# Last two sequences staged like the others, last unit's gates put off, and the first weight loads and transposes reordered, in an attention and mixture-of-experts kernel on one core

## Chip, core and metric

The kernel runs on one core of a Trainium2 chip. The metric is the time of one execution in microseconds (us) on the device. The kernel before was timed in three runs: 684.95, 686.94 and 687.5 us, median 686.94 us. A profiled execution of it took 678.78 us.

Names used below: PE is TensorE (matmuls and transposes; PEld is its weight load), DVE is VectorE, ACT is ScalarE, POOL is GpSimd, SP is SyncE, which here only issues DMAs. ACT and POOL issue DMAs as well.

## What is computed

Input x has 8 sequences of 512 tokens with 256 features, all in f32. The reference, cut to what matters:

```
x = x + attention(layernorm(x))
x = x + ffn(layernorm(x))

attention(x): q = x Wq; k = x Wk; v = x Wv
  scores = where(causal, q k^T, -inf)
  return softmax(scores / sqrt(256)) v

ffn(x): shared = (silu(x sg^T) * (x su^T)) sd^T            # 512 hidden
  probs = sigmoid(x router^T + bias)                       # 8 experts
  scores, indices = top_k(probs, 2); scores /= sum(scores)
  combined = sum over the two experts of score * expert(x) # same form as shared
  return shared + combined
```

So every token goes through causal attention within its sequence, through one shared expert, and through 2 of 8 routed experts.

## The kernel before, in words

**Order of the work.** `fold_qk` (L280 to L313) first loads Wq and Wk, transposes them on PE (L297, copied out by ACT at L298) and multiplies them (L307), so that scores are x (Wq Wk^T) x^T. Then the loop `for b in range(B)` (L630) does the sequences. In its stage, sequence b gets its attention products and second normalisation, and in the same stage the scores and values of sequence b+1 are computed (pm of L395 and L407, sc of L442) and the routing of sequence b is done. Then come the routed experts (`expert_up` L888, matmuls L900; `expert_down` L918, matmuls L923) over tiles of rows that were gathered by expert, and last the sums.

**Attention of one chunk.** A sequence has four chunks of 128 queries. `attend` (L458) takes the exponentials of a chunk transposed and multiplies them with v (`av`, L472), adds the result to the residual (`summed`, on DVE, L476, out `total`), and takes the statistics (L172 to L178 on DVE, `rstd` on POOL, L179); `normalize` (L325) writes the rows `hn` of the chunk before.

**Two ways of transposing.** PE can transpose a 128x128 block against the identity (L463 for the exponentials `ex`, `turned` with L340 for rows of hn), and ACT copies the result from PSUM to SBUF. Or SP writes the rows to DRAM, loads them back as blocks or squares of 32 (`stored_rows`, `loaded_blocks`, `loaded_squares`), and DVE transposes the blocks (`turn_squares` L384, `turn_exponentials` L434). Which sequence goes which way is set by three constants:

- `VIA = [b for b in range(B) if b != B - 2]`: their hn goes through DRAM, at least the first half.
- `WHOLE = range(B - 2)`: the second half of hn goes through DRAM too.
- `SENT = range(1, B - 1)`: their exponentials go through DRAM.

So before the change the hn of sequences 0 to 5 goes through DRAM, that of sequence 6 is transposed by PE, that of sequence 7 half and half, and the exponentials of sequences 0 and 7 are transposed by PE. `LATE` are sequences 4 to 6, whose shared expert is done at the end of the kernel from a copy of hT in DRAM (`hTd`).

**Units of the shared expert.** `shared_beside` (L564) does one unit: half a sequence, with 16 gate and up matmuls (pg, L578), the activation (tanh on ACT, two products on DVE at L593 and L596) and 8 down matmuls (po, L605). In the profile each of these matmuls is two rows. The units of sequences 0 to 3 and of sequence 7, ten in all, fill PE where the attention would make it wait. Before the change one unit lies in each of the stages of sequences 0 to 5, one beside the last sequence's routing (`added`), and three come after it and before the routed experts.

**Routing.** `chosen` (L754) holds a sequence's routing in steps, which `shared_beside` calls at the places named in `steps`: `turned` for what PE transposes, then `route` (L486): logits `lT` (L492), their transpose `pl` (L500), sigmoid, two maxima with their masks, and running counts `run` (L535). `places_of` (L540, PE at L544 and L545, out `pp`, then DVE to `at`, L554) gives each token its row, and `dispatch` (L557) writes a chunk's rows to `rows_h` by indirect DMAs from POOL, eight in each sequence.

**What sets the order.** `tc.issue_after(x)` puts the instructions below it behind x in the order of the program; on one engine they are then queued behind x. It adds no wait of its own. Each engine runs its queue in order, and buffers do the rest: `ps_o` has two PSUM buffers for lT, pl, po, av and pp, `ps_m` four for pm, sc and pg, `ps_t` two for transposes.

**The routed experts' inputs.** `fetch_w` (L831) loads the expert weights from ACT's queue, `fetch` (L841) the tiles `h` (L851) and `tail` (L856) from SP's queue; the first of these waits until the last dispatch has landed. `turn` (L873) transposes h on DVE for L900.

## Time and profile before

| What | Value |
|---|---|
| median of the timed runs | 686.94 us (684.95 to 687.5) |
| profiled execution, time | 678.78 us |
| profiled execution, span of the core | 677.0 us |
| DVE busy | 301.9 us (45%) |
| POOL busy | 157.2 us (23%) |
| ACT busy | 149.6 us (22%) |
| gate and up matmuls of routed experts, L900 | 896 rows, 211.6 us |
| down matmuls of routed experts, L923 | 448 rows, 101.4 us |
| gate and up matmuls of the units, L578 | 320 rows, 73.8 us |
| all DMA traffic | 119.52 MB, mean 177 GB/s |

The profile is one execution on the chip. A row of a group has the line, the engine, the operation, out<-in by the program's names, the shape and the count; then the busy time and the mean of one. A row of a timeline starts with its start in us from the span's start and its length; in brackets stands how long the engine was idle before it, and what ended that. Matmul rows overlap a little, since they are pipelined, so the cost of a row is better read from one start to the next.

### The profile page before, as it was taken

How to read it: one execution, taken by the hardware profiler on the slowest of the kernel's cores; microseconds unless marked ns; L12 is line 12 of the kernel's file. 1: busy time of each engine (PE TensorE's matmuls, PEld its weight loads, DVE VectorE, ACT ScalarE, POOL GpSimd, SP SyncE). 2: the span in 40 equal slices, each digit the busy share in tenths (PEclk: the TensorE clock that was granted, in tenths of full speed). 3: DMA queues.
4: the chain of work that ended last, by engine and by line, in shares of the span. 5: the costliest groups of instructions: out<-in, count | busy, mean ns of one | idle time of the engine just before them, and what ended most of it. 6: DMA issues, size and time to landing. Idle time of an engine off the chain costs nothing.

```text
span 677.0 us, 10380 instructions
## 1 busy us (share of the span) xinstructions
PE 663.7 (98%) x3170; PEld 542.0 (80%) x3170; DVE 301.9 (45%) x1004; ACT 149.6 (22%) x357; POOL 157.2 (23%) x210
## 2 busy tenths in 40 slices
PE   7999999999999999999999999999999999999998
PEld 5677787777776888888888888888888899984556
DVE  4678879779786853212212212122122112223665
ACT  3433231332223222121111111211111111111110
POOL 3103351533526520022112121111211122120000
PEclk9999999999999999999999999999999999999999
DMA  7665777867834367776555354463543457714775
GB/s 237 192 166 147 219 210 178 220 180 209 218 115 134 106 163 226 230 199 209 162 167 170 119 180 150 138 180 127 161 161 102 159 172 239 259 65 146 244 226 177
DMA packets 155529, 119.52 MB, mean 177 GB/s; under 512 B 111856, under 2 KB 134000, under 8 KB 155472
## 3 DMA queue, kind: packets, MB, share of 16 engines
q1 hardware_dynamic: 136272, 58.05, 32.8%
q10 hardware_dynamic: 12912, 43.53, 18.5%
q0 software_dynamic: 6288, 17.24, 7.0%
q8 instruction: 28, 0.46, 0.3%
q14 instruction: 29, 0.24, 0.1%
HBM read 83.31 MB, written 35.47 MB: 175 GB/s over the span
## 4 chain that ended last, share of the span: by engine, by line
PE 78%; DVE 9%; DMA 6%; SPq 2%; issue 2%; POOL 1%; ACT 1%; ACTq 0%; DVEq 0%; POOLq 0%
PE po L923 17%; PE pg L900 16%; PE pu L900 16%; PE pg L578 7%; PE po L605 4%; PE pg L1011 3%; PE po L1070 3%; PE pu L1011 3%; PE av L472 3%; PE sc L442 2%; PE pm L407 2%; PE pm L395 2%; SPq L377 2%; DVE bnst L172 2%; DMA blocks<-hnd 2%
## 5 line engine op out<-in xcount | busy, mean ns | idle before, releaser
L886 DVE TENSOR_TENSOR hidp<-pu,sgt 128x512 f32<-128x512 f32 x56 | 38.5, 690 | 209.2 <-PE pu L900 194.4
L929 POOL DMA_INDIRECT rows_y<-y,to x56 | 53.6, 957 | 263.7 <-ACT y L928 155.2
L900 PE MATMUL pg<-hTt,w 128*128 128x256 f32 x448 | 105.8, 379 | 0.0
L900 PE MATMUL pu<-hTt,w 128*128 128x256 f32 x448 | 105.8, 379 | 0.0
L923 PE MATMUL po<-w_down,hidp 128*128 x448 | 101.4, 379 | 0.9 <-ACT y L928 0.9
L923 PEld LDWEIGHTS po<-w_down,hidp 128*128 128x128 f32 x448 | 85.0, 190 | 12.8 <-ACT y L928 1.4
L900 PEld LDWEIGHTS pg<-hTt,w 128*128 128x128 f32 x448 | 85.1, 190 | 11.6
L900 PEld LDWEIGHTS pu<-hTt,w 128*128 128x128 f32 x448 | 85.1, 190 | 11.6
L578 PE MATMUL pg<-hT,w_sh 128*128 128x256 f32 x320 | 73.8, 382 | 0.2 <-issue 0.2
L559 POOL DMA_INDIRECT rows_h<-hn,at x64 | 62.9, 983 | 22.7 <-issue 17.1
L885 ACT ACTIVATE sgt<-pg 128x512 f32<-128x512 f32 x67 | 39.8, 598 | 125.8 <-PE pg L900 122.2
L578 PEld LDWEIGHTS pg<-hT,w_sh 128*128 128x128 f32 x320 | 59.7, 190 | 9.5 <-ACT sg L589 1.0
L928 ACT COPY y<-po 128x256 f32<-128x256 f32 x67 | 24.9, 373 | 156.0 <-PE po L923 142.9
L179 POOL TENSOR_TENSOR rstd<-var,minus_half 128x1 f32<-128x1 f32 (+1 forms) x43 | 27.0, 636 | 125.7 <-DVE var L178 77.1
L605 PE MATMUL po<-w_sh,hid 128*128 128x256 f32 x160 | 37.5, 384 | 0.2
L442 PE MATMUL sc<-xT,qT 128*128 128x128 f32 (+3 forms) x128 | 37.4, 434 | 0.0
L605 PEld LDWEIGHTS po<-w_sh,hid 128*128 128x128 f32 x160 | 29.2, 190 | 6.8 <-DVE hid L596 2.5
L395 PE MATMUL pm<-xT,w_qk 128*128 128x512 f32 x64 | 30.1, 592 | 0.0
L886 DVE TENSOR_TENSOR khid<-pu,sgt 128x512 f32<-128x512 f32 x11 | 7.6, 691 | 49.2 <-PE pu L900 49.2
L407 PE MATMUL pm<-wv_sb,xT 128*128 128x256 f32 x128 | 29.0, 380 | 0.2 <-ACT xT L341 0.2
L407 PEld LDWEIGHTS pm<-wv_sb,xT 128*128 128x128 f32 x128 | 24.2, 190 | 6.1 <-issue 2.6
L172 DVE BATCH_NORM_STATS2 bnst<-total 128x6 f32<-128x256 f32 x64 | 25.1, 409 | 8.3 <-DMA total<-in_x_dram 8.3
(156 smaller groups left out, 755.7 us busy)
## 6 DMA issues: line engine op xcount, KB each, us to landing
w<-in_gate_w_dram ACTq DMA_DIRECT2D x41, 512.0 KB, 3.4
w<-in_up_w_dram ACTq DMA_DIRECT2D x41, 512.0 KB, 4.7
yl<-rows_y SPq DMA_DIRECT2D x32, 256.0 KB, 4.0
h<-rows_h SPq DMA_DIRECT2D x112, 64.0 KB, 3.3
w_down<-in_down_w_dram SPq DMA_DIRECT2D x8, 512.0 KB, 4.6
out_dram<-total SPq DMA_DIRECT2D x32, 128.0 KB, 2.7
total<-in_x_dram SPq DMA_DIRECT2D x7, 512.0 KB, 7.0
hnd<-hn SPq DMA_DIRECT2D x13, 256.0 KB, 2.2
```

What stands on the lines that cost most here:

```text
L395: nc.tensor.matmul(pm, lhsT=w_qk[:, k, ts(m, P)], rhs=xT[:, k, :], start=(k == 0), stop=(k == ND - 1),)
L407: nc.tensor.matmul(pm, lhsT=xT[:, k, ts(c, P)], rhs=wv_sb[:, k, :], start=(k == 0), stop=(k == ND - 1),)
L442: nc.tensor.matmul(sc[:, :n], lhsT=qT[:, k, ts(i, P)], rhs=xT[:, k, :n], start=(k == 0), stop=(k == ND - 1),)
L559: lands(nc.gpsimd.indirect_dma_start(out=rows_h[:, :], out_offset=bass.IndirectOffsetOnAxis(ap=at[:, r, c : c + 1], axis=0), in_=hn[:, c, ...
L578: mm = nc.tensor.matmul(pg[:, w, :], lhsT=w_sh[:, ds(w * gu + k * I + m * P, P)], rhs=hT[:, k, at], start=(k == 0), stop=(k == ND - 1),)
L605: nc.tensor.matmul(po, lhsT=hid[:, m, ts(j, P)], rhs=w_sh[:, ds(2 * gu + m * D, D)], start=(m == 0), stop=(m == NI - 1),)
L885: nc.scalar.activation(sg, pg, AF.Silu)
L886: return nc.vector.tensor_tensor(out=hid, in0=pu, in1=sg, op=ALU.mult).ins
L900: nc.tensor.matmul(dst[:, m, :], lhsT=w[:, i, k, ts(m0 + m, P)], rhs=hT[:, ts(k, n * P)], start=(k == 0), stop=(k == ND - 1),)
L923: nc.tensor.matmul(po, lhsT=hid[:, m, ts(j, P)], rhs=w_down[:, ds(w + m * D, D)], start=(m == 0), stop=(m == NI - 1),)
L929: nc.gpsimd.indirect_dma_start(out=rows_y[:, :], out_offset=bass.IndirectOffsetOnAxis(ap=to[:, j : j + 1], axis=0), in_=y, in_offset=None,)
L1011: nc.tensor.matmul(dst, lhsT=w_sh[:, ds(off + k * I + m * P, P)], rhs=hT[:, k, :], start=(k == 0), stop=(k == ND - 1),)
```

## The change

The change has four parts.

1. The three constants become `range(7)`, `range(7)` and `range(1, 8)`: hn of sequence 6 and the exponentials of sequence 7 go through DRAM and DVE like those of the others, and hn of sequence 7 is transposed wholly by PE. With this the stage of sequence 6 has the same order as those before it: its normalisation, its second maximum, its steps of routing and a unit of the shared expert. `project_q` is skipped where there is no next sequence, and the last sequence keeps `placed` at chunk 2. One of the ten units lies in the stage of sequence 6 now, so that two instead of three are left after the last routing.
2. The unit beside the last sequence has its gates on DVE put behind the last `summed` (`gates_behind`), and the matmuls behind the first pair of it are put behind the last av (`halfway` moves from the place (1, 1) to (0, 1)).
3. The first half of the columns of Wk is loaded from ACT's queue instead of SP's. SP then has the first half of Wq and goes on with x; ACT has the second half of Wq and both halves of Wk.
4. PE does the four transposes of Wq first and then the four of Wk, instead of two and two in turn.

```diff
--- before.py
+++ after.py
@@ -73,9 +73,9 @@
     assert B == E, "each sequence's attention has one expert's down weights loaded beside it"
     EARLY = B // 2
     LATE = range(EARLY, B - 1)
-    VIA = [b for b in range(B) if b != B - 2]
-    WHOLE = range(B - 2)
-    SENT = range(1, B - 1)
+    VIA = range(B - 1)
+    WHOLE = range(B - 1)
+    SENT = range(1, B)
 
     BLOCKS = NT * (NT - 1) // 2, NT
     RS = 1.0 / D ** 0.5
@@ -283,7 +283,8 @@
             for n, w in (("q", wq), ("k", wk)):
                 t = beside.tile([P, ND, D], F32, tag="hT", name=f"w{n}", bufs=3)
                 loaded.append(t)
-                for k, queue in enumerate((nc.sync, nc.scalar)):
+
+                for k, queue in enumerate((nc.sync if n == "q" else nc.scalar, nc.scalar)):
                     columns = ts(k, P)
                     queue.dma_start(
                         out=t[:, :, columns], in_=w.rearrange("(p c) e -> p c e", c=ND)[:, :, columns]
@@ -294,9 +295,11 @@
                 pt = ps_t.tile([P, ND, D], F32, tag="t", name="pt")
                 for k in range(ND):
                     for c in range(ND):
-                        begun = nc.tensor.transpose(pt[:, k, ts(c, P)], t[:, c, ts(k, P)], ident).ins
+                        with nullcontext() if n == "q" else tc.issue_after(turned_q):
+                            begun = nc.tensor.transpose(pt[:, k, ts(c, P)], t[:, c, ts(k, P)], ident).ins
                     copied = nc.scalar.copy(tT[:, k, :], pt[:, k, :])
                 if n == "q":
+                    turned_q = begun
                     with tc.issue_after(copied.ins):
                         nc.scalar.dma_start(out=wv_sb, in_=wv.rearrange("(p c) e -> p c e", c=ND))
                 turned.append(tT)
@@ -479,7 +482,7 @@
             stats_of(mv, xb[:, i, :], i)
             power = rstd_of(rstd[:, i : i + 1], mv[:, i : i + 1, :])
             if i:
-                with tc.issue_after(summed.ins) if i != NT // 2 or xb is not total[B - 1] else nullcontext():
+                with tc.issue_after(summed.ins):
                     normalize(hn[:, i - 1, :D], xb, i - 1, mv, rstd)
             return mixed.ins, summed.ins, power
 
@@ -510,7 +513,7 @@
                 top, hot = tops[r][:, here], hots[r][:, here, :]
                 if r:
                     yield
-                with tc.issue_after(marks["turned"]) if r and b < B - 2 else nullcontext():
+                with tc.issue_after(marks["turned"]) if r and b < B - 1 else nullcontext():
                     nc.vector.tensor_reduce(out=top, in_=prob, axis=AX.X, op=ALU.max)
                 nc.vector.tensor_tensor(
                     out=hot, in0=prob, in1=top.unsqueeze(2).to_broadcast(wide), op=ALU.is_equal
@@ -561,7 +564,7 @@
                     in_=hn[:, c, :], in_offset=None,
                 ))
 
-        def shared_beside(b, half, hT, midway=None, behind=None, rows_from=NI, early=None, steps=(), halfway=None):
+        def shared_beside(b, half, hT, midway=None, behind=None, rows_from=NI, early=None, steps=(), halfway=None, gates_behind=None):
 
 
             n = S // 2
@@ -583,13 +586,14 @@
                         with tc.issue_after(mm.ins):
                             next(early, None)
                             held = marks["routed"]
-                    elif (m, w) == (NI // 2 - 1, 1) and halfway is not None:
+                    elif (m, w) == (0, 1) and halfway is not None:
                         held = halfway
                 sg = beside.tile([P, n], F32, tag="sg", name="sg")
                 nc.scalar.activation(sg, pg[:, 0, :], AF.Tanh, scale=0.5)
-                with nullcontext() if early is None or not 0 < rows_from < NI and m < rows_from else tc.issue_after(
-                    marks["half"] if m >= rows_from else marks["coming"]
-                ):
+                first = marks["half"] if m >= rows_from else marks["coming"]
+                if early is None or not 0 < rows_from < NI and m < rows_from:
+                    first = gates_behind
+                with nullcontext() if first is None else tc.issue_after(first):
                     nc.vector.scalar_tensor_tensor(
                         out=sg, in0=sg, scalar=1.0, in1=pg[:, 0, :], op0=ALU.add, op1=ALU.mult
                     )
@@ -661,7 +665,7 @@
                 rest = None
                 if b in SENT:
                     sc = exs[i]
-                    if i % 2 == 0:
+                    if i % 2 == 0 and ahead_T is not None:
                         with tc.issue_after(mixed) if i else nullcontext():
                             qT = project_q(ahead_T, range(i // 2 * ND // 2, (i // 2 + 1) * ND // 2), qT if i else None)
                 elif i + 1 < NT:
@@ -692,7 +696,7 @@
                     with tc.issue_after(summed):
                         added()
                     added = None
-                if i == (1 if b in SENT else 2) and placed is not None:
+                if i == (1 if b in SENT and ahead_T is not None else 2) and placed is not None:
                     placed()
 
 
@@ -760,7 +764,7 @@
                 next(routing)
                 yield
                 next(routing)
-                if b < B - 2:
+                if b < B - 1:
                     yield
                 mask = next(routing)
 
@@ -773,11 +777,8 @@
             if b + 1 < B:
                 choice = chosen()
                 next(choice)
-                if b + 2 == B:
-                    for _ in choice:
-                        pass
             else:
-                added = shared_beside(*waiting.pop(0), early=chosen(), rows_from=0, halfway=mixed, steps=((NI // 2, 1), (NI - 1, 0), (NI - 1, 1)))
+                added = shared_beside(*waiting.pop(0), early=chosen(), rows_from=NI, halfway=mixed, gates_behind=summed, steps=((NI // 2, 1), (NI - 1, 0), (NI - 1, 1)))
             if b in LATE:
                 with tc.issue_after(marks["sent"]):
                     nc.sync.dma_start(out=hT_d[b], in_=hT)
@@ -785,27 +786,26 @@
                 waiting += [(b, 0, hT), (b, 1, hT)]
             if b + 1 < B:
 
-                if b + 2 < B:
-                    def behind():
-
-                        nonlocal exT
-                        with tc.issue_after(marks["hid"]), tc.issue_after(marks["first"]):
-                            exT = turn_exponentials(squares)
-                        next(choice, None)
-                        marks["squares"], marks["turned"] = marks["turned"], marks["run"]
-
-                    def midway():
-                        if b + 3 < B:
-                            with tc.issue_after(marks["squares"]):
-                                rows, _ = first_norm(*coming)
-                            with tc.issue_after(marks["sent"]):
-                                blocks[b + 3], _ = sent_to_blocks(xn_d[b + 3], rows)
-
-                    added = shared_beside(
-                        *waiting.pop(0), midway=midway, behind=behind, early=choice,
-                        rows_from=1 if b in WHOLE else NI,
-                        steps=((NI // 2, 1), (NI - 1, 1)) if b in WHOLE else ((0, 1), (1, 1)),
-                    )
+                def behind():
+
+                    nonlocal exT
+                    with tc.issue_after(marks["hid"]), tc.issue_after(marks["first"]):
+                        exT = turn_exponentials(squares)
+                    next(choice, None)
+                    marks["squares"], marks["turned"] = marks["turned"], marks["run"]
+
+                def midway():
+                    if b + 3 < B:
+                        with tc.issue_after(marks["squares"]):
+                            rows, _ = first_norm(*coming)
+                        with tc.issue_after(marks["sent"]):
+                            blocks[b + 3], _ = sent_to_blocks(xn_d[b + 3], rows)
+
+                added = shared_beside(
+                    *waiting.pop(0), midway=midway, behind=behind, early=choice,
+                    rows_from=1 if b in WHOLE else NI,
+                    steps=((NI // 2, 1), (NI - 1, 1)) if b in WHOLE else ((0, 1), (1, 1)),
+                )
                 xT = ahead_T
         placed()
         for c in to_send:
```

## The prediction

> **What bounds the kernel now.** I read the page's first lines, then the waits of TensorE (PE), then the timeline of PE from 170 us to 290 us (where the change works) beside VectorE (DVE), GpSimd (POOL) and SyncE (SP), and last the first 13 us.
>
> The first line of the page and its row of granted clock:
>
> ```profile
> PE 663.7 (98%) x3170; PEld 542.0 (80%) x3170; DVE 301.9 (45%) x1004; ACT 149.6 (22%) x357; POOL 157.2 (23%) x210
> PEclk9999999999999999999999999999999999999999
> ```
>
> PE is the bound: 663.7 of 677.0 us. All its idle time is 13.3 us, so a change can win only by taking PE work out or by emptying some of these 13.3 us, and it loses where PE gets a new wait. The waits of PE (total us, times, longest):
>
> ```profile
> PE pt L297 <- DMA wq<-in_wq_dram: 4.0, 1, 4.0
> PE po L923 <- ACT y L928: 0.9, 1, 0.9
> PE pt L463 <- ACT ex L451: 0.7, 2, 0.4
> PE pl L500 <- ACT logits L497: 0.4, 1, 0.4
> PE pp L545 <- DVE run L535: 0.3, 1, 0.3
> PE lT L492 <- ACT hT L341: 0.2, 1, 0.2
> ```
>
> The last four stand in the stage that the change rewrites (sequence 7 under the routing of sequence 6, 198 to 217 us): by the timeline 0.20 + 0.39 + 0.31 + 0.39 = 1.29 us. The rest of the idle time is outside it. From PE's timeline (start, us, operation):
>
> ```profile
> 198.06 0.61 PE L442 MATMUL sc<-xT,qT 128*128 128x128 f32 x4
> 201.96 1.10 PE L340 MATMUL pt<-ident,hn 128*128 128x128 f32 x8
> 203.26 0.43 PE L492 MATMUL lT<-hT,r_sb 128*32 128x128 f32 x8 [0.20 <-ACT hT L341]
> 214.26 0.66 PE L463 MATMUL pt<-ident,ex 128*128 128x128 f32 x4 [0.39 <-ACT ex L451]
> 217.48 3.62 PE L578 MATMUL pg<-hT,w_sh 128*128 128x256 f32 x16
> 255.97 3.62 PE L605 MATMUL po<-w_sh,hid 128*128 128x256 f32 x16
> 259.42 1.89 PE L900 MATMUL pg<-hTt,w 128*128 128x256 f32 x8
> ```
>
> 217.48 is where the last attention product ends; call it T0. 259.42 is the first routed expert. Between them PE has only shared units (half a sequence of the shared expert), the last sequence's transposes and its routing. From start to start a row of 128x256 costs 0.216 us, a unit (32 pg rows, 16 po rows) 6.91 + 3.45 = 10.36 us.
>
> **The change, part by part.**
>
> 1. *Transposes.* The four groups of L463 go (start to start 0.26, 0.28, 0.33, 0.49: 1.36 us); the eight of sequence 6's hn go (1.10); sequence 7's hn takes eight instead of four (+0.47, the four at 220.93 to 221.40). Sum **-1.99 us** of PE work. In their place come DVE transposes and SP's transfers: hnd, four blocks, two exd, eight squares, one hTd. DVE is busy 45% and does the same for sequences 1 to 5 without a PE wait, so I put them at 0.
>
> 2. *The four waits go* as the stage becomes like that of sequence 5, where PE never idles: **-1.29**.
>
> 3. *What is late next.* Sequence 5's stage, from sc at 170.85 to pl at 186.30, is 15.45 us; call the start of pl P. After it, in sequence 7, PE has pl and 16 po rows (0.11 + 3.45), 8 pg rows (1.73), av of chunks 0 and 1 (6 rows, 1.30): ready for chunk 2 at P + 6.6. The old stages have two pm groups here (1.72 each); sequence 7 has no next sequence to project, so this cover is gone. av, pp, lT, pl and po share two PSUM buffers (ps_o), so chunk 2 needs the buffer of chunk 0, freed by `summed`. DVE in sequence 5's stage:
>
> ```profile
> 192.17 0.77 DVE L535 TENSOR_TENSOR run<-run,mask 128x8 f32<-128x8 f32 x4
> 192.86 0.48 DVE L476 SCALAR_TENSOR_TENSOR total<-av,inv,total 128x256 f32<-128x256 f32 x1
> 193.32 0.48 DVE L476 SCALAR_TENSOR_TENSOR total<-av,inv,total 128x256 f32<-128x256 f32 x1
> 196.16 0.41 DVE L325 TENSOR_SCALAR hn<-total,mv,rstd 128x256 f32<-128x256 f32 x1 [0.42 <-POOL rstd L179]
> 196.89 0.48 DVE L476 SCALAR_TENSOR_TENSOR total<-av,inv,total 128x256 f32<-128x256 f32 x1
> ```
>
> The first `summed` stands behind the second routing maximum and `run`, and ends at 193.34 = P + 7.04: a wait of **+0.46** for chunk 2 (then 1.30, to P + 8.34). pp follows (0.36; the last sequence has `placed` at chunk 2), to about P + 8.8, and chunk 3 needs the buffer of chunk 2, whose `summed` stands in DVE's order behind two bnst, var, POOL's rstd and normalise of chunk 0: in these rows it ends at 197.37, 0.61 of it a wait for pp and 0.4 the place operations, which come later now: about P + 10.1. That is **+1.3** for chunk 3. Both waits: +1.8; bounds 0 (if DVE is through in time, as in the old stages) and 2.5 (with the pp wait of 0.61 as well). Behind the waiting av stand on PE only shared matmuls, so no other engine loses more than PE.
> T0 is then 198.06 + 15.45 + 10.1 + 1.73 = 225.3.
>
> 4. *The unit moved.* It lies in sequence 6's stage now, so from T0 to the first routed expert PE has 41.94 - 10.36 + 0.47 = **32.05 us** of work: the routed stage would begin at 225.3 + 32.05 = 257.4, which is 2.0 earlier than 259.42. But the first routed tile has a chain of its own, which ran beside this cover:
>
> ```profile
> 223.90 0.27 PE L500 MATMUL pl<-ident,logits 128*128 128x128 f32 x1
> 231.81 0.96 POOL L559 DMA_INDIRECT rows_h<-hn,at  x1 [4.23 <-DVE at L554]
> 241.15 0.96 POOL L559 DMA_INDIRECT rows_h<-hn,at  x1 [0.30 <-issue]
> 247.05 1.96 SPq L851 DMA_DIRECT2D h<-rows_h  x4
> 257.38 1.29 DVE L873 STREAM_TRANSPOSE hTt<-h 128x512 f32<-128x512 f32 x2
> ```
>
> Last dispatch at T0 + 23.7, its landing lets SP fetch h at T0 + 29.6, the rows had landed by T0 + 33.5 (251.0: DVE then had other work first), and one transpose of 0.65 and its handover make T0 + 34.4. Before, PE came at T0 + 41.9: 7.5 us to spare. After, it comes at T0 + 32.05. The chain moves little: pl comes 0.3 to 0.4 later (8 transposes, not 4, are ahead of it), DVE's way from pl to `at` is shorter by 0.2 as the gates stand elsewhere; sequence 6's eight dispatches now all stand ahead of these (8 x 1.27 = 10.2 us from about T0 + 3) and are out at T0 + 13.2, just before T0 + 14.3. So PE waits **+2.4** at L900, where it waited for nothing; bounds: 0 (the last dispatch lands in 3.0 us, the fastest of the eight, instead of 5.9) and 8 (it takes 7.6, and h 7.8, the slowest of the routed stage, instead of 3.95). 2.4 is the row's own case.
>
> 5. *The gates put off, the order of normalise and the second maximum.* DVE has the same operations in another order; the price is in 3 and 4. For gates put behind `summed`, hid comes later, but the po rows that need it come after lT and pl: 0.
>
> 6. *Routed stage.* At 283.90 ScalarE (ACT) was held 7.45 us by a weight issue that waited for an h landing, and PE by 0.95. The transfers' order ahead of it shifts; I take half, **-0.5** (-0.95 to +1, another stall of that size).
>
> 7. *Start.* One Wk half leaves SP (0.83 us at 1.50), so x0 is issued 0.87 earlier; but it becomes the third on ACT (0.66 + 0.62 ahead of it) and lands, with the 3.80 us it took, near 5.9 instead of 5.3. wq's four transposes fill 4.0 to 5.3, wk's four end near 7.2, and the fold ends near 9.4, where PE now waits for xn anyway (9.42). **0**, bounds -0.8 (x0's gain in full) and +0.6 (wk's delay in full).
> [...]
>
> *Sum against the profiled run:* -1.99 - 1.29 + 1.8 = -1.5 by terms; the pieces of 3 and 4 give -2.0 (the stage of sequence 7 had another 0.5 of changeover between kinds of rows that sequence 5's has not), and I use these. -2.0 + 2.4 - 0.5 + 0 = **-0.1 us**. The profiled run took 678.78 us (span 677.0), 8.2 below the median of 686.94; I carry the difference over: **686.8 us**.
>
> [...]
>
> **The rivals.**
>
> *A, faster: the new waits don't come.* For it: sequences 1 to 5 run so without idle, and DVE's order is loose by half a us here and there. Against it: two PSUM buffers and no pm between. If chunk 2 and 3 find their buffers and h lands in time: -2.0 - 1.8 - 0.5 = -4.3, **682.6**. Chance 0.14.
>
> *B, slower: the chain to the first routed tile grows.* It decides as soon as the chain exceeds the cover of 32.05 us after T0: from there each us counts in full. Its place is the landing of the last dispatch and of h; 16 dispatches stand in one row on POOL instead of 14 with a gap, beside eight fills of rows_h and the expert weights. For it: landings of dispatches here vary from 3.0 to 7.6 us. At the slow end, 8 instead of 2.4: -0.1 + 5.6 = +5.5, **692.4**. Chance 0.16.
>
> *C, the exponentials of sequence 7 come late* (exd, eight squares, two DVE transposes of 1.57 in all ahead of av). In sequence 5 they start 0.02 us after DVE's operation before them, so nothing was late. If they are late by one landing of exd (2 to 3 us), +2.5: **689.3**. Chance 0.14.
>
> **How the numbers follow.** Forecast 686.8 with 0.56; A 0.14, C 0.14, B 0.16. A measurement of this kernel can tell about 0.5% (3.4 us) from no change. A alone is faster by more than that, B alone slower; forecast and C lie within: 0.14, 0.70, 0.16. Range: from 683.2, near A, to 690.8, which takes in C and half of B.
>
> **What would show it.** PE's 22 transposes of L463 and L340 for sequences 6 and 7 become 8; the four old waits are gone; av at L472 of the last sequence waits for DVE `total` about 0.5 and 1.3 us; pg at L900 has a wait of about 2.4 for DVE hTt. Wrong if: av waits for nothing (A), L900 waits over 5 us (B), or av waits for exTs (C). A changed start shows as another time of L407, 10.73 now.

## The result, and the profile after

The changed kernel takes 687.48 us (median of 11 runs) beside 685.40 us for the kernel before in the same comparison: ratio 1.0042, 95% interval 1.0025 to 1.0059. By the ratio it is slower by 2.9 us (the medians differ by 2.1), where no change (-0.1 us) was forecast. Two further comparisons gave 1.0063 (1.0041 to 1.0085) and 1.0053 (1.0029 to 1.0077).

One thing must be known to read what follows. The runs fell on several chips, of two kinds: on two of them the median of the kernel before is 684.8 and 686.8 us, on two others 678.7 and 678.9. The profile shown with the prediction is of the second kind and the times beside it of the first; this is where the 8 us between them come from. I call the chips *late* and *prompt*; part 4 of the experiments shows why. Profiles are compared within a kind.

The first profile of the changed kernel (late chip, span 687.4 us) has these first lines on its page:

```profile
span 687.4 us, 10367 instructions
PE 667.4 (97%) x3156; PEld 541.0 (79%) x3156; DVE 304.7 (44%) x1003; ACT 147.6 (21%) x356; POOL 157.0 (23%) x210
```

PE has 3156 rows instead of 3170: the 14 transposes are gone, and PE still bounds the kernel. Its waits (total us, times, longest):

```profile
PE pp L547 <- DVE mask L533: 3.5, 1, 3.5
PE pg L900 <- ACT sgt L885: 1.8, 1, 1.8
PE av L475 <- DVE total L479: 1.6, 2, 1.0
PE pg L900 <- DVE hTt L873: 1.5, 1, 1.5
```

A second profile of the same kernel, on a prompt chip (after_again, span 680.2 us; the kernel before beside it 677.0 us):

```profile
PE pg L900 <- DVE hTt L873: 2.5, 1, 2.5
PE pg L900 <- ACT sgt L885: 1.5, 1, 1.5
PE av L475 <- DVE total L479: 1.4, 2, 1.0
PE pp L547 <- DVE mask L533: 0.3, 1, 0.3
```

The four old waits of the stage are gone in both. The forecast waits are there: av for DVE's `total` (1.4, forecast 1.8) and the first pg of L900 for hTt (2.5, forecast 2.4). The wait for ACT's sgt was not forecast at all, and the wait for mask is large on the late chip alone (part 4 of the experiments shows why). Where the time went, from the starts of rows in the traces (sc7 is the first sc of sequence 7, T0 the end of its last av, both as in the prediction):

| stretch, us | before | after | change | forecast |
|---|---|---|---|---|
| prompt: sc7 to T0 | 19.43, 19.43 | 27.33, 27.50 | +8.0 | +7.9 |
| prompt: T0 to first L900 | 41.94, 41.94 | 35.03, 34.63 | -7.1 | -7.5 |
| prompt: first L900 to PE's end | 412.86, 413.06 | 414.91, 415.20 | +2.1 | -0.5 |
| prompt: sum | 474.3 | 477.3 | +3.0 | -0.1 |
| late: sc7 to T0 | 23.31 | 27.89 | +4.6 | |
| late: T0 to first L900 | 44.21 | 39.31 | -4.9 | |
| late: first L900 to PE's end | 413.11 | 415.23 | +2.1 | |
| late: sum | 480.6 | 482.4 | +1.8 | |

(Prompt: the second and third profile of each kernel; late: one execution of each, from two comparisons.) The sums hold the whole change: sc7 itself starts at 197.8 to 199.5 us in the prompt profiles of both kernels. On the prompt chips the forecast holds within 0.5 us up to the first routed tile, where +0.9 us was measured and +0.4 forecast. The other 2.1 us of the loss lie behind it, and they are there on both kinds of chip.

How they come about, on the prompt chip. ACT's timeline of after_again, first tiles of the routed stage:

```profile
261.43 0.34 ACTq L838 DMA_DIRECT2D w<-in_gate_w_dram  x1
265.01 0.34 ACTq L838 DMA_DIRECT2D w<-in_up_w_dram  x1
267.71 0.34 ACTq L838 DMA_DIRECT2D w<-in_gate_w_dram  x1
268.22 0.34 ACTq L838 DMA_DIRECT2D w<-in_up_w_dram  x1
268.59 1.28 ACT L885 ACT_TABLE_LOAD   x1 [8.81 <-DMA w<-in_up_w_dram]
269.89 1.08 ACT L885 ACTIVATE sgt<-pg 128x512 f32<-128x512 f32 x2
```

ACT issues the weights of tiles 2 and 3 before it may work on tile 0, since that is its queue's order. In the traces these issues wait for landings of tile 1's h, with which they share DMA semaphores: in the changed kernel's first profile three of them start at 271.05, 274.71 and 275.43 us, 0.02 to 0.03 us after the last landing of an h transfer on the same semaphore (271.03, 274.69 and 275.40). In the kernel before, h was fetched from 247 us on, and all six issues went out from 260.2 to 263.5. Of its first profile:

```profile
260.20 0.34 ACTq L838 DMA_DIRECT2D w<-in_gate_w_dram  x1
263.45 0.37 ACTq L838 DMA_DIRECT2D w<-in_up_w_dram  x1
263.85 1.28 ACT L885 ACT_TABLE_LOAD   x1 [3.85 <-DMA w<-in_gate_w_dram]
265.15 0.60 ACT L885 ACTIVATE sgt<-pg 128x512 f32<-128x512 f32 x1
```

Now h is fetched from 257.18 on, at the time of the issues, and ACT is held 8.81 us. PE and SP of after_again:

```profile
261.85 1.99 PE L900 MATMUL pg<-hTt,w 128*128 128x256 f32 x8 [2.50 <-DVE hTt L873]
270.54 1.99 PE L900 MATMUL pg<-hTt,w 128*128 128x256 f32 x8 [1.51 <-ACT sgt L885]
```
```profile
257.18 1.99 SPq L851 DMA_DIRECT2D h<-rows_h  x4
```

PE first waits 2.50 us for h, then its four ps_m buffers are full of tile 0's pg and pu, and it waits 1.51 us more for sgt. Four such buffers last PE some 6.9 us (four groups of 8 rows, 1.73 each); the first sgt starts 5.7 us after the first L900 in the kernel before and 8.0 us after it here. My reading is that both waits have one cause: the work that covered the chain got some 10 us shorter (a unit of 10.36 less, four transposes of 0.47 more). unit_twice below tests it.

### The profile page after: what moved, and what is told of

It is laid out like the page before. It is cut to its first block, busy times and chain, and to the rows that moved or that the text cites. A ratio compares the mean times of both kernels' runs of the same rounds, so it can differ in the third digit from the quotient of the medians.

```text
span 687.4 us, 10367 instructions
## 1 busy us (share of the span) xinstructions
PE 667.4 (97%) x3156; PEld 541.0 (79%) x3156; DVE 304.7 (44%) x1003; ACT 147.6 (21%) x356; POOL 157.0 (23%) x210
## 4 chain that ended last, share of the span: by engine, by line
PE 87%; DVE 4%; DMA 3%; SPq 2%; issue 2%; ACT 1%; another core or an unknown queue 1%; POOL 0%; ACTq 0%; DVEq 0%; POOLq 0%
PE po L923 17%; PE pg L900 16%; PE pu L900 16%; PE pg L581 7%; PE sc L445 4%; PE av L475 4%; PE pm L410 4%; PE pm L398 3%; PE pg L1011 3%; PE po L1070 3%; PE pu L1011 3%; PE po L609 3%; PE lT L495 1%; DMA h<-rows_h 1%
## 5 line engine op out<-in xcount | busy, mean ns | idle before, releaser
L900 PE MATMUL pg<-hTt,w 128*128 128x256 f32 x448 | 106.0, 379 | 3.3 <-ACT sgt L885 1.8
L900 PE MATMUL pu<-hTt,w 128*128 128x256 f32 x448 | 105.8, 379 | 0.0
L923 PE MATMUL po<-w_down,hidp 128*128 x448 | 101.3, 379 | 0.0
L900 PEld LDWEIGHTS pg<-hTt,w 128*128 128x128 f32 x448 | 85.0, 190 | 15.6 <-ACT sgt L885 2.2
L900 PEld LDWEIGHTS pu<-hTt,w 128*128 128x128 f32 x448 | 85.1, 190 | 11.6
L923 PEld LDWEIGHTS po<-w_down,hidp 128*128 128x128 f32 x448 | 85.0, 190 | 11.5
L581 PE MATMUL pg<-hT,w_sh 128*128 128x256 f32 x320 | 75.8, 389 | 0.4 <-ACT v L414 0.4
L885 ACT ACTIVATE sgt<-pg 128x512 f32<-128x512 f32 x67 | 39.9, 597 | 128.0 <-PE pg L900 113.8
L475 PE MATMUL av<-v,exTs 128*128 128x256 f32 x140 | 33.4, 384 | 1.6 <-DVE total L479 1.6
L475 PEld LDWEIGHTS av<-v,exTs 128*128 128x128 f32 x140 | 26.0, 190 | 7.8 <-issue 2.9
L592 ACT ACTIVATE sg<-pg 128x256 f32<-128x256 f32 x40 | 14.7, 384 | 70.2 <-PE pg L581 28.3
```

The source lines that it names most:

```text
L475: mixed = nc.tensor.matmul(av, lhsT=exT[:, ts(j, P)], rhs=v[:, j, :], start=(j == 0), stop=(j == i))
L581: mm = nc.tensor.matmul(pg[:, w, :], lhsT=w_sh[:, ds(w * gu + k * I + m * P, P)], rhs=hT[:, k, at], start=(k == 0), stop=(k == ND - 1),)
L885: nc.scalar.activation(sg, pg, AF.Silu)
L900: nc.tensor.matmul(dst[:, m, :], lhsT=w[:, i, k, ts(m0 + m, P)], rhs=hT[:, ts(k, n * P)], start=(k == 0), stop=(k == ND - 1),)
L923: nc.tensor.matmul(po, lhsT=hid[:, m, ts(j, P)], rhs=w_down[:, ds(w + m * D, D)], start=(m == 0), stop=(m == NI - 1),)
```

## The experiments

Ratios are to the kernel before, timed beside it, with the 95% interval. Diffs are cut to the lines that matter.

**1. Both kernels again, and the start by itself.** start_undone makes this edit in the changed kernel; start_only makes the reverse of it in the kernel before:

```diff
-                for k, queue in enumerate((nc.sync if n == "q" else nc.scalar, nc.scalar)):
+                for k, queue in enumerate((nc.sync, nc.scalar)):
-                        with nullcontext() if n == "q" else tc.issue_after(turned_q):
-                            begun = nc.tensor.transpose(pt[:, k, ts(c, P)], t[:, c, ts(k, P)], ident).ins
+                        begun = nc.tensor.transpose(pt[:, k, ts(c, P)], t[:, c, ts(k, P)], ident).ins
```

> The kernel before, unchanged, for a second profile. Theory (the change costs its time in the last routing): this profile is like the first, span 677 to 679 us, logits (L497) start 0.05 us after lT's last row in every stage. Rival (the two profiles fell in different states of PE's signals, and most of the 10.4 us between them is not the change): span 683 to 686 us, and logits start 1.0 to 1.7 us after lT from the second stage on, as in the profile of the changed kernel. Time 0.0 against before by both.

> The changed kernel, unchanged. Both theories: +2 to +3 us against before. Theory: the profile has the 3.5 us wait of PE (pp on DVE's mask) and the 3.4 us at half clock behind it again. Rival: that wait came of late signals; where logits follow lT by 0.05 us, ACT's eviction of sh follows its po at once, and PE waits 0.6 us or less there.

> The changed kernel with the loads of Wk and the transposes at the start as before. Theory (the start costs): av of the first sequence is 0.75 us earlier than in the changed kernel (27.5 instead of 28.2 us), and the time falls from +2.5 to about +1.7 us against before. Rival (the start is worth nothing, as forecast): within 0.3 us of the changed kernel.

> The kernel before with the new start alone. Theory: +0.8 us (+0.3 to +1.3) against before. Rival: 0.0, within 0.3.

Measured, all on one prompt chip: before_again 1.0001 (0.9988 to 1.0014), span 677.0; after_again 1.0063; start_undone 1.0058 (1.0040 to 1.0076); start_only 0.9998 (0.9986 to 1.0009). So the start is worth nothing, as forecast; the 0.75 us by which the first sequence's av was later in the first profile (28.21 instead of 27.46 us) do not show in the time; in three profiles of the kernel before alone that row starts at 27.45 to 29.06. The theory that the 3.5 us wait for mask belongs to the change fell: it is 0.3 us here. The change costs some 4 us here all the same.

**2. Four edits of the changed kernel, on a late chip.** more_cover moves one more sequence's shared expert ahead of the routed experts:

```diff
-    LATE = range(EARLY, B - 1)
+    LATE = range(EARLY + 1, B - 1)
-    before_next = [2 * NI + NT, NI, len(early) - 3 * NI - NT]
+    before_next = [2 * NI + NT, len(early) - 2 * NI - NT]
```

(with four buffers for hT instead of three)

> The changed kernel with sequence 4's shared expert done in two units before the routed experts instead of at the end (LATE one shorter, a fourth buffer for hT, the sums shared out over two late sequences). That puts 20.7 us of PE work more between the last attention product and the first routed expert. Theory (the time is lost because the cover of 32 us is shorter than the chain to the first routed tile, and the weights' issues then meet the h transfers): PE's waits of 2.5 us at the first pg of L900 and of 1.5 us behind ACT's first sgt both go; about 4 us better than the changed kernel, so +0 us against before (to +3 if the end, with two late sequences over which to lay the sums, gets longer). Rival (the waits come from the order of queues alone, whatever the cover): both waits stay, and the time is that of the changed kernel, +3.5 to +4.5.

Measured 1.0276 (1.0247 to 1.0304). Both waits are gone, as the theory has it, but another stands at L900 and the end is worse than I allowed for:

```profile
PE pg L900 <- DMA w<-in_gate_w_dram: 4.1, 1, 4.1
```

The span is 18.0 us longer than that of the changed kernel's first profile (705.4 against 687.4), of which 10.3 lie after PE's last row: 13.7 us of sums and stores (705.4 - 691.7) instead of 3.4. As a test of the cover it is unclear; unit_twice below does it better.

mask_first:

```diff
-        added()
+        with tc.issue_after(marks["placed"]):
+            added()
```

> The changed kernel with the last unit's sum (total at L815, 0.68 us on DVE, between hot and mask of the last routing) put behind the last place operations. Theory (each us of that chain counts in full): the wait at the first pg of L900 falls from 2.5 to about 1.8 us, the wait of pp for mask (0.3) goes, 0.7 us better than the changed kernel: +3 us against before. Rival (the chain is set by POOL or the DMAs, not by DVE): no change in the wait, +3.6 to +4.3.

Measured 1.0096 (1.0065 to 1.0126): slower than the changed kernel on a chip of this kind (1.0042). The large wait for mask is gone and L900 comes 2.9 us sooner after T0 (36.38 instead of 39.31), but ACT is then held 10.7 us ahead of its first sgt, and PE waits for that:

```profile
PE pg L901 <- ACT sgt L886: 4.4, 1, 4.4
```

Here a chain that got shorter, without the queue behind it being cleared, paid in the next wait.

gate_first takes those issues out of ACT's way:

```diff
-            items += [fetch(t)[1] for t in range(1, AHEAD)]
+            items += [fetch(t)[1] for t in range(1, AHEAD - 1)]
-            if t + AHEAD <= MEAN:
+            if t and t + AHEAD <= MEAN:
             hid, product = expert_up(t, w, hT, kept_hid[t % 2] if t >= PAIRS else None)
+            if t == 0:
+                with tc.issue_after(gates[-1]):
+                    items += [fetch(s)[1] for s in (AHEAD - 1, AHEAD)]
```

(gates holds the activations of L885)

> The changed kernel with the fetches of routed tiles 2 and 3 (their h from SP's queue and their weights from ACT's) put behind the two activations of tile 0. Theory (ACT's weight issues waited for h landings and held sgt): PE's wait of 1.5 us for sgt goes, the wait of 2.5 at the first pg of L900 stays, 1.5 us better than the changed kernel: +2.2 us against before; if tile 2 then comes late, a wait for w or h stands there instead. Rival (the hold only moves to the next activation): +3.6 to +4.3.

Measured 1.0041 (1.0026 to 1.0057). The wait for sgt is gone; the time is not better. The mean granted clock of its profile is 0.994, that of the changed kernel's first 0.997: by an estimate from these and the spans, some 8 us at half clock instead of some 4. Over the timed runs it is 0.995 or less in 8 of 12, and in 5 of the 11 of the changed kernel. That this is where the gain went is likely, not shown.

gates_undone:

```diff
-rows_from=NI, halfway=mixed, gates_behind=summed, steps=
+rows_from=0, halfway=mixed, steps=
-                    elif (m, w) == (0, 1) and halfway is not None:
+                    elif (m, w) == (NI // 2 - 1, 1) and halfway is not None:
```

> The changed kernel with the second part undone: the last unit's gates where they were, and its first eight pg matmuls, not four, ahead of the last av. Theory (that part is worth little): DVE has two products for each pg ahead of summed; the waits of av for DVE grow by 0 to 1.5 us in all, and the time is within -0.5 and +1.5 us of the changed kernel. Rival (putting the gates off is what lengthens the last routing's chain): the wait at L900 falls by 1 us or more and the time gets better by as much.

Measured 1.0110 (1.0084 to 1.0135), beyond what I expected. Without the second part one wait of av alone is longer than both were:

```profile
PE av L475 <- DVE total L479: 3.1, 1, 3.1
```

and sc7 to T0 takes 32.59 us instead of 27.89: four pg matmuls that now stand ahead of T0 (8 rows, 1.7 us), 1.5 us more of waiting, and some 1.5 us that I put down to the clock, an estimate. The rival is right in that the waits at L900 fall (for hTt from 1.5 to 0.6 us, for sgt from 1.8 to none) and wrong in the rest: the last `at` is written 18.65 us after T0 with and without the second part, so putting the gates off did not lengthen that chain, and the time got worse. By the ratios (1.0110 and 1.0042, from two comparisons) the second part saves some 4.7 us on a late chip. Part of that is clock: its mean is 0.992 in this profile and 0.997 in the changed kernel's first, by an estimate from these and the spans some 11 us at half clock against some 4. No prompt chip was tried.

**3. Again, and both edits together, on a prompt chip.** mask_gate_first has the edits of mask_first and gate_first; dispatch_later puts sequence 6's dispatches behind sequence 7's:

```diff
-                if b in SENT:
+                if b == B - 1:
+                    now = 0
+                elif b in SENT:
+        held_back = [(sent, c) for c in to_send]
         placed()
         for c in to_send:
             dispatch(*sent, c)
+        with tc.issue_after(ready[-1]):
+            behind_all = nc.gpsimd.memset(spacer, 0.0).ins
+        with tc.issue_after(behind_all):
+            for those, c in held_back:
+                dispatch(*those, c)
```

> The kernel before, unchanged, for a third profile. Theory (a chip on which the kernel before takes some 685 us has late signals from PE while POOL's dispatches run; one on which it takes some 679 us has not): if the time is near 685 us, logits start over 1 us behind lT from the second stage on, as in the first profile of the changed kernel; if it is near 679 us, 0.05 us. Rival (the late signals belong to the changed kernel): 0.05 us in either case.

> The changed kernel, unchanged. Theory: where logits follow lT by 0.05 us, the waits of the second profile come again (L900 for hTt 2.5, for sgt 1.5, mask 0.3) and the time is +3.5 to +4.5 us against before; where logits are late by 1 us and more, those of the first (mask 3.5, sgt 1.8, hTt 1.5) and +2 to +3.5 us.

> The changed kernel with both edits: the last unit's sum behind the last place operations, and the fetches of tiles 2 and 3 behind the activations of tile 0. Theory (the chain to the first routed tile and ACT's queue each have their own price): no wait for mask, none for sgt, 1.5 to 2 us at the first pg of L900, clock 1.0 there: 2 us or more better than the changed kernel, so +1.5 us or less against before. Rival (each wait taken away comes back in the next): +3 us or more.

> The changed kernel with sequence 6's eight dispatches on POOL put behind sequence 7's eight, so that none runs during the last lT, pl and po. The last dispatch is some 10 us later. Theory for the chain: the first pg of L900 waits some 10 us instead of 2.5 (1.5), and the time is +11 to +16 us against before, with a stretch at half clock. Theory for the signals: on a chip with late signals, ACT's sh of that unit follows its po at once (under 0.2 us instead of 2.8) and PE's wait for mask falls from 3.5 to 0.5 us or less; if dispatches have no part in it, they stay late.

Measured: before_third 1.0007 (0.9988 to 1.0026); after_third 1.0053, with the waits of the second profile again (hTt 2.1, sgt 1.8, av 1.4, mask 0.3); mask_gate_first 1.0022 (1.0004 to 1.0040), that is 1.5 us slower than before instead of 3.6; dispatch_later 1.0195 (1.0163 to 1.0227), 13 us, within what was expected. Of mask_gate_first:

```profile
PE pg L901 <- DVE hTt L874: 1.7, 1, 1.7
PE av L475 <- DVE total L479: 1.4, 2, 1.0
PE pp L547 <- DVE mask L533: 0.2, 1, 0.2
```

The wait for sgt is gone, and first L900 to PE's end is 413.54 us instead of 415.1: the hold of ACT is worth 1.5 us there. In dispatch_later the last dispatch stands 10.2 us later after T0 (33.85 instead of 23.68), and PE pays for it at the place that was named:

```profile
PE pg L909 <- DVE hTt L882: 10.5, 1, 10.5
```

**4. The cover itself, av's wait, and the late signals, on a late chip.** unit_twice does one shared unit twice and leaves the second result unused; norm_mask_gate puts, in the last sequence, chunk 0's normalisation behind the third summed, on top of mask_gate_first:

```diff
+        shared_beside(*waiting[0])
         while waiting:
```
```diff
-            if i:
+            if i and (i > 1 or xb is not total[B - 1]):
                 with tc.issue_after(summed.ins):
+                    if i == NT // 2 and xb is total[B - 1]:
+                        normalize(hn[:, 0, :D], xb, 0, mv, rstd)
                     normalize(hn[:, i - 1, :D], xb, i - 1, mv, rstd)
```

> The changed kernel with one shared unit computed twice, its second result unused: 10.4 us of PE work more between the last attention product and the first routed tile. Theory (the cover is too short by 2 to 2.5 us and the weights' issues meet the h transfers): the wait at the first pg of L900 goes, that for sgt too, and the time rises by 10.4 - 2.3 - 1.5 = 6.5 us only, so +10 us against before (9 to 11.5). Rival (the waits are of the queues' order, not of the cover): both waits stay and the time rises by all 10.4 us, +14 us against before.

> The changed kernel with both earlier edits (the last unit's sum behind the place operations, the fetches of tiles 2 and 3 behind the activations of tile 0), and with the normalisation of chunk 0 of the last sequence behind the third summed instead of ahead of it. Theory (chunk 3's av waits for that summed, which waits for POOL's rstd): the wait of av falls from 1.4 to 0.5 us, T0 is 0.9 earlier with the chain behind it, and the time is 0.9 us better than with the two edits: +0.5 us against before (-0.5 to +1.5). Rival (the wait goes to another buffer, or the chain to the first routed tile does not move with T0): no better than with the two edits, +1.5 us.

> The kernel before, unchanged, one look. Theory (late signals are of the chip): on a chip where the kernel before takes some 685 us, logits follow lT by over 1 us from the second stage on and by 0.05 in the first; where it takes some 679 us, by 0.05 throughout. Rival: 0.05 throughout on either.

> The changed kernel with sequence 6's dispatches behind sequence 7's, unchanged from the earlier run, one look. Theory for the signals: on a chip of the late kind, logits of sequence 7 and sh of the unit beside them follow PE at once (under 0.2 us), since no dispatch runs there, while the stages before, with dispatches, keep their 1 us and more. Rival: late there too.

unit_twice: 1.0136 (1.0120 to 1.0152), +9.3 us. PE got 10.36 us more to do, and the kernel got 6.4 us slower than the changed one (1.0042, +2.9) is. In the whole list of PE's waits there is none at L900 any more; these are its largest:

```profile
PE pt L299 <- DMA wq<-in_wq_dram: 4.0, 1, 4.0
PE pp L547 <- DVE mask L533: 3.8, 1, 3.8
PE pg L581 <- issue: 2.0, 5, 0.7
PE av L475 <- DVE total L479: 1.5, 2, 1.0
```

And first L900 to PE's end is 411.32 us against 415.23. Of these 3.9 us the wait for sgt is 1.8; some 1.5 are a wait at the down matmuls late in the routed stage (L923), which every other profile has (1.3 to 2.1 us, the kernel before too) and this one has not; why is open. So both waits come of the cover, and the rival that they are of the queues' order alone is wrong.

norm_mask_gate: 0.9995 (0.9980 to 1.0011), no difference from the kernel before (its profile is of the slowest of its 12 runs). av's wait falls to 0.8 us (1.5 in unit_twice on that chip) and sc7 to T0 to 27.45 us (27.97). It is the best version found, and it does not beat the kernel before. Since mask_gate_first was not run on a late chip, how much of this the last edit gives is open.

before_fourth (one run, 687.72 us) has the late signals as well, also in the stages that the change leaves alone. PE and ACT of its fifth stage, then of the last routing of dispatch_later2 (one run, 697.69 us), same chip, where no dispatch runs:

```profile
157.80 0.81 PE L578 MATMUL pg<-hT,w_sh 128*128 128x256 f32 x3
158.54 1.10 PE L492 MATMUL lT<-hT,r_sb 128*32 128x128 f32 x16
160.36 0.66 ACT L589 ACTIVATE sg<-pg 128x256 f32<-128x256 f32 x2 [3.95 <-PE lT L492]
160.91 0.27 ACT L497 COPY logits<-lT 128x128 f32<-128x128 f32 x1
```
```profile
237.36 0.64 PE L495 MATMUL lT<-hT,r_sb 128*32 128x128 f32 x16
238.13 0.27 ACT L500 COPY logits<-lT 128x128 f32<-128x128 f32 x1 [0.93 <-PE lT L495]
241.44 0.38 ACT L613 ACTIVATE sh<-po 128x256 f32<-128x256 f32 x1 [1.77 <-PE po L609]
```

In the first, lT ends at 159.64 and logits start 1.26 us later. They stand behind two sg activations, and those are late themselves: the pg rows ahead of lT had ended at 158.61, and ACT, idle for 3.95 us, started at 160.36. In the second, logits start 0.13 us after lT's end at 238.00. Of the first profile of the changed kernel, with dispatches running from 232.4 to 242.4 us:

```profile
236.50 3.94 PE L609 MATMUL po<-w_sh,hid 128*128 128x256 f32 x16
243.16 0.38 ACT L613 ACTIVATE sh<-po 128x256 f32<-128x256 f32 x1 [5.32 <-remote]
244.31 0.69 DVE L815 TENSOR_TENSOR total<-total,sh 128x512 f32<-128x512 f32 x1 [2.95 <-ACT sh L613]
```

There the first sh starts 2.7 us after the last of the po rows; in dispatch_later2, without dispatches, 1.2 us before it (the first sh needs only a part of them), as on a prompt chip (after_again). DVE's mask stands behind the sum that waits for sh. With sh in time PE's wait for mask is 0.3 us in dispatch_later2, where it is 3.5 to 4.2 us in the other profiles of the changed kernel on late chips that keep that sum ahead of mask. So POOL's dispatches have a part in the late signals, and the signals make the wait for mask. That they belong to the chip is not shown: on the late chip where both kernels were profiled both have them, and on the prompt ones neither, but each chip was used for one batch of runs only.

## Why the prediction was wrong

*Right.* The transposes (14 rows of PE fewer) and the four old waits went (points 1 and 2). T0 came 27.3 to 27.5 us after sc7, forecast 27.28; av waited 0.35 and 1.02 us, forecast 0.46 and 1.3 (point 3). The wait at L900 was 2.5 and 2.1 us, forecast 2.4; the last dispatch stood at T0 + 23.67, as forecast, and h was fetched at T0 + 29.9 to 30.3, forecast 29.6 (point 4). That the gates put off cost nothing (point 5) is right and too modest: by gates_undone the second part saves some 4.7 us on a late chip. The start is worth 0 (point 7, runs 0.9998 and 1.0058 against 1.0063).

*Wrong: point 6,* "I take half, -0.5 (-0.95 to +1, another stall of that size)". It measured +2.1 (+0.8 against the first profile alone, from which the term was taken). Two things were amiss in it. The 0.95 us that I counted on winning was in the first profile of the kernel before only: there first L900 to PE's end took 414.22 us, in the second and third 412.86 and 413.06. And the row that I quoted, ACT held by a weight issue that waits for an h landing, told what the change would do with it: point 4 has h fetched at the time at which ACT issues the weights, and I did not carry that from point 4 to point 6. The hold went from the third tile, where PE had work in hand, to ahead of the first sgt, where it had four buffers. mask_gate_first takes it away and is 1.5 us shorter in this stretch; gate_first takes it away too, but without a better time; unit_twice takes it away by cover alone. PE's wait for sgt is 1.5 and 1.8 of the 2.1 us in the two prompt profiles; the rest was not traced to a row. So point 6 is off by 2.6 us; with 0.4 us more of chain and 0.1 of T0 this is the difference of 3.1 us between the forecast -0.1 and the measured +3.0.

*The rivals.* A did not come (av and L900 waited). B's place and point of decision were right, its price was not: the chain was 34.6 to 35.0 us on prompt chips, not 40 (39.3 on the late one, where L900 still waits only 1.5 us for hTt); what it added came behind L900. C did not come: no av waited for exTs.

*The range* held the time, and the change's sign was missed: the working put gains of 3.8 us and losses of 4.2 us against each other and had no margin for a term that appears only once the cover is gone. That 686.8 us lies so near the measured 687.48 is luck: it was counted from 686.94 us, the median of three runs, and the kernel before took 685.40 beside the changed one. It is luck too that points 3 and 4, worked out from a prompt profile, nearly fit in sum on late chips, where the first comparison ran: the two stretches changed by +4.6 and -4.9 us there, not by +7.9 and -7.5.

*The row of granted clock* that the prediction shows has a 9 in every slice. It says nothing of the first us: the trace's record of the clock begins 8.4 us after the start (10.4 us in the changed kernel's first profile). The rows of PE do. Of the first profile of the kernel before, behind waits of 4.01 us for wq and 0.67 for wk:

```profile
6.97 2.62 PE L307 MATMUL pm<-wkT,wqT 128*128 128x256 f32 x8
10.73 3.72 PE L407 MATMUL pm<-wv_sb,xT 128*128 128x256 f32 x16 [0.20 <-ACT xT L341]
```

The first rows of the fold start 0.43 us apart (6.97, 7.40, 7.82, 8.25), those from 8.56 us on (8.56, 8.78, 8.99, 9.21) and the rows of L407 0.216: PE begins at half of its later rate. In the changed kernel's first profile all eight rows of the fold start 0.43 us apart, from 7.07 to 10.06.

## What to carry to other kernels

A change that takes work from in front of a hand-over takes cover from every transfer that ran under it (here PE got waits of 2.5 and 1.5 us at L900, in after_again): price not only the first tile's arrival but also what those transfers now meet, here the issues of the next weights on an engine that computes as well. A DMA issue that waits in a compute engine's queue is a stall of that engine (ACT was held 8.81 us in after_again): look at what it waits for and what stands behind it. A gain that rests on a stall seen in one profile should be counted only if a second profile has it too.

## What had not been expected of the hardware

*Late signals.* In the changed kernel's first profile, on a late chip, logits start 1.01 to 1.71 us after the end of lT in the second to the seventh stage and 0.56 us in the last; in all of these POOL's indirect DMAs run beside lT or just ahead of it. On another late chip it is 1.26 us in the fifth stage of before_fourth and 2.04 us in that of dispatch_later2. On prompt chips it is 0.05 to 0.07 us in all eight stages of the first profile of the kernel before, and 0.13 us in the last of after_again. Where no dispatch ran, logits came in time on the late chips too (0.07 us in the first stage of the changed kernel's first profile, 0.13 in the last routing of dispatch_later2). The stage of sequence 7 of the kernel before takes 23.31 us on a late chip and 19.43 on a prompt one; a wait of 2.6 us at av (before_fourth) is a part of that. By what path the dispatches delay them is not settled.

*The clock.* The profile by windows of the changed kernel's first profile (start:end, length, busy us and count of PE, PEld, DVE, ACT, POOL, then granted clock, DMA share, GB/s), a stretch with the 3.5 us wait for mask, and of dispatch_later, with the wait of 10.5 us from 259.3 to 269.8:

```profile
240.00:248.00 8.00, 4.48 (x20) 3.67 (x19) 3.97 (x24) 1.15 (x3) 1.92 (x2) 0.87 0.15 52
```
```profile
263.00:267.00 4.00, 0.00 (x0) 0.00 (x0) 0.00 (x0) 0.00 (x0) 0.00 (x0) 0.65 0.29 78
267.00:271.00 4.00, 1.17 (x3) 1.00 (x4) 1.29 (x2) 0.00 (x0) 0.00 (x0) 0.50 0.89 196
271.00:280.00 9.00, 9.00 (x36) 7.62 (x35) 1.91 (x4) 2.48 (x3) 0.00 (x0) 0.81 0.99 274
```

After 3.5 us of waiting the clock was at half for 3.4 us (245.9 to 249.3, granted 0.50), after 10.5 us until some 274.4, by the 0.81 of the last stretch: 4.6 us into the new work. Shorter waits went both ways. Behind the one of 2.6 us in before_fourth two sc rows of 128x512 take 1.71 us to the next row's start (217.12 to 218.83), where the same two take 0.86 in the first profile of the kernel before (209.47 to 210.33). In after_again and after_third, with waits of 2.5 and 2.1 us at L900, the mean granted clock is 1.000. What decides is not shown.
